# Moving an elementwise product from VectorE to GpSimd in a four-layer graph network

## The chip, the cores and the metric

The kernel runs on one core of a Trainium2 chip. The engines of a core work side by side, each on its own queue of instructions: TensorE (PE in the profile; PEld is its loading of weights), VectorE (DVE), ScalarE (ACT), GpSimd (POOL), and SyncE (SP), which here issues transfers. They meet through semaphores and through on-chip memory: SBUF, with 128 partitions, and PSUM, where TensorE leaves its results. GpSimd works on SBUF alone in this kernel. The metric is the time on the device in microseconds (us), the median of several runs; lower is better.

## The reference, cut to what matters

For 32 graphs of 512 nodes with 64 features, four layers are applied one after another, each as x = layernorm(x + layer(x, adj)). Layer 0 is a mean over neighbours; layer 1 a Chebyshev filter of order 4; layer 2 a hyperbolic attention over all pairs of nodes; layer 3 a quantile aggregation over the neighbours with an MLP. The change lies in layer 2:

```python
x_local = logmap(x_i, x_j, c)                  # for every pair of nodes
logits = einsum('bijk,ko->bijo', feats, att_W)[..., 0] + att_b[0]
att = sigmoid(logits) * adj
support_t = einsum('bij,bijd->bid', att, x_local)
return proj(expmap(support_t, x, c), c)
```

The adjacency adj is a 512 x 512 matrix for each graph with values between 0.05 and 1 at some entries and 0 elsewhere. logmap(x_i, x_j) is a weight for the pair times a combination of x_i and x_j, so layer 2 comes down to a matrix of pair weights, which is multiplied elementwise with the adjacency and with the sigmoid, and then to a product of this matrix with x.

## The kernel before, in words

A graph is one batch. Its 512 nodes lie as T = 4 tiles of P = 128 partitions, so that a 512 x 512 matrix is a tile [128, 4, 512]: four row blocks of 512 columns. Each batch goes through stages that the kernel calls lanes: `front` (line 1000: loading, transposing the adjacency into AT, layers 0 and 1), `pairs` (line 1086: layer 2's pair matrix), `tail` (from line 1211, the rest of layer 2 and its normalization), `graph` (line 996: sizes and ranks of neighbourhoods for layer 3), `gather` (line 1270: one-hot matrices and TensorE products that gather the neighbours' values), `sort` (line 1368: a sorting network of minima and maxima on VectorE, tiles SB and SH), and `head` (line 1399: quantiles, MLP, output). `head` works on two batches at once.

The order of all instructions is made while the program is built. Each helper (`tt`, `ts`, `stt` for VectorE, `act` for ScalarE, `mm` and `tr` for TensorE, `gtt` and `gts` for GpSimd) does not issue anything; it records an operation with `seq.op(engine, issue, tail, ...)`: its engine, the time that it is taken to hold the engine, and the time until its result can be used, with dependencies found from the regions that it reads and writes. Then `issue` (line 361) runs a list scheduler over all 32 batches. Each engine has a planned clock; among the operations that are ready on an engine, the one with the smallest due time goes first. The due time (`due`, line 334) is the batch number plus a number of periods, times a period of 80 us; that number is read from the knots in `STAGES` (line 1536), by how deep the operation lies in its lane's chain. So the entries of `STAGES` spread the lanes of a batch over time and set which of several lanes an engine serves first. Between operations of different engines the plan adds `HOP + LATE` (0.05 + 0.08 us). The resulting order is fixed for each engine; what waits at run time waits on semaphores. Helpers record every operation, so the profile shows the line of the helper: L514 is any `tensor_tensor` on VectorE, L521 any `scalar_tensor_tensor`, L518 any `tensor_scalar`, L550 any activation, L537 and L541 narrow arithmetic on GpSimd, L813 a power -0.5 on GpSimd, L582 an indirect gather that GpSimd issues, L1280 a fill on GpSimd. The tile names tell them apart.

In `pairs`, the matrix Q (tile pairs_Q) holds a symmetric function of each pair, L the logits and their sigmoid, Wt the final weights:

- for each row block i, TensorE writes a product into a PSUM bank; `stt` on VectorE (line 1193) multiplies it with Q[:, i] into L[:, i], and ScalarE applies the sigmoid;
- then VectorE multiplies Q in place with AT, in two instructions of 2 x 512 columns (lines 1195 to 1197). The first needs the first two row blocks of L to be done with Q, the second the last two;
- for each row block j, TensorE transposes L into a PSUM bank, and `stt` (line 1203) multiplies it with Q[:, j] into Wt[:, j];
- TensorE multiplies Wt with x and its companions, and the lane `tail` follows.

GpSimd's work in the kernel is narrow: chains of operations on tiles of 128 x 4 (one value per node) in `pairs` and `tail`, the powers for normalizations, descriptors for the gathers of layer 3, and fills of padding.

Of the kernel before, what the change touches and what calls it, by code (L numbers as in the profile page):

```python
# [15 lines left out]
OP = mybir.AluOpType  # L16
# [223 lines left out]
class Order:  # L240
# [3 lines left out]

    ENGINES = ("PE", "DVE", "ACT", "POOL", "SP")
    HOP = 0.05
    LATE = 0.08
    STAY = 58.8

    def __init__(self, nc, tc):  # L250
# [103 lines left out]
    def after(self, d, i, end, full):  # L354

        a, b = self.ops[d], self.ops[i]
        if a[0] == b[0]:
            return end + (a[2] if full and a[0] != "PE" else 0.0)
        return end + a[2] + self.HOP + self.LATE

# [109 lines left out]
def tile_adj_resnorm(ctx: ExitStack, tc: tile.TileContext, x, adj, nodemask, w1k, b1k, att_w, att_b,  # L470
                     w1, b1, w2, b2, out):
    nc = tc.nc
    B, N, D = x.shape
    T = N // P
# [16 lines left out]
    seq = Order(nc, tc)  # L491
# [7 lines left out]
    def vec(f, out, ins, one=False, scalars=(), reads=None, **kw):  # L499

        n = width(reads if reads is not None else out)
        tiles = [out] + list(ins)
        rate = 1.04e-3
        if not any(a.space == PSUM for a in tiles):
            half = all(a.dtype in (F16, BF16) for a in tiles)
            if one:
                rate = 0.26e-3 if half else 0.52e-3
            elif half:
                rate = 0.52e-3
        sc = [a for a in scalars if isinstance(a, bass.AP)]  # L510
        seq.op("DVE", 0.07 + n * rate + 0.065 * len(sc), 0.085, f, [out], list(ins) + sc)

    def tt(out, a, b, op):
        vec(lambda: nc.vector.tensor_tensor(out, a, b, op=op), out, [a, b])  # L514
# [28 lines left out]
    def act(out, a, f, bias=None, scale=1.0, accum_out=None, after=None):  # L543
        sc = [x for x in (bias, scale) if isinstance(x, bass.AP)]
        kw = {k: v for k, v in (("bias", bias), ("accum_out", accum_out)) if v is not None}
        n = width(out)
        table = "exp" if f in (AF.Ln, AF.Exp) else "sig" if f in (AF.Sigmoid, AF.Tanh) else None
        near = 0.06 if a.space == PSUM else 0.1
        seq.op("ACT", near + n * 0.83e-3 + 0.09 * len(sc) + (0.09 if accum_out is not None else 0.0),
             0.1, lambda: nc.scalar.activation(out, a, f, scale=scale, **kw), [out, accum_out], [a, after] + sc, table)  # L550
# [535 lines left out]
    def pairs(b, res):  # L1086

        mid = pools["mid"]
        AT, FL = res["AT"], res["FL"]
# [88 lines left out]
        Q = seq.tile(mid, [P, T, N], F32, "Q", 1)  # L1178
# [11 lines left out]
        for i in range(T):  # L1190
# [1 line left out]
            mm(pt, FT[:D + 3, 1, i * P:(i + 1) * P], FT[:D + 3, 2, :], start=True, stop=True)  # L1192
            stt(L[:, i, :], pt, 0.5, Q[:, i, :], op0=OP.mult, op1=OP.mult)
            act(L[:, i, :], L[:, i, :], AF.Sigmoid, bias=oo[:, i:i + 1])
        for g in range(2):
            gs = slice(2 * g, 2 * g + 2)
            tt(Q[:, gs, :], Q[:, gs, :], AT[:, gs, :], op=OP.mult)
        Wt = seq.tile(mid, [P, T, N], F32, "Wt", 1, "RW")
        for j in range(T):
            pt = bank()  # L1200
# [304 lines left out]
    def within_bounds():  # L1505

        gm, BT = pools["gm"], B * T
        seq.lane = "graph"
        p1, p2, p3 = bank(), bank(), bank()
        ge = [seq.tile(gm, [P, T, N], F16, "ge", 1, t).rearrange("p t n -> p (t n)") for t in ("nbT", "v")]  # L1510
        ge = [ge[s % 2][:, s // 2 * BT:(s // 2 + 1) * BT] for s in range(K + 1)]
        seq.lane = "check"
        m = M3.rearrange("p b t -> p (b t)")

        for s in range(K + 1):
            ts(ge[s], m, float(s), None, op0=OP.is_gt)
        for s in range(K + 1):
            mm(p1[:BT, s:s + 1], ge[s], onesP[:, 0:1], start=True, stop=True)
        cs = seq.tile(gm, [BT, K + 1], F16, "cs")
        act(cs, p1[:BT, :K + 1], AF.Copy)  # L1520
        mm(p2[:B, :K + 1], graphs[:BT, :], cs, start=True, stop=True)
        off = seq.tile(gm, [B, 2, K + 1], F16, "off")
        for i, op in enumerate((OP.is_gt, OP.is_lt)):
            tt(off[:, i, :], p2[:B, :K + 1], limits[:, i, :], op=op)
        bad = seq.tile(gm, [B, 1], F32, "bad")
        reduce(bad, off.rearrange("p i s -> p (i s)"), OP.max)
        badh = seq.tile(gm, [B, 1], F16, "badh")
        cp(badh, bad)
        mm(p3[:1, 0:1], badh, onesP[:B, 0:1], start=True, stop=True)
        ts(flag, p3[:1, 0:1], 0.0, None, op0=OP.is_gt)  # L1530
# [2 lines left out]

    STAGES = {"front": (-0.67, -0.59, -0.59, -0.4, -0.35), "pairs": (1.01, 1.02, 1.54, 1.44, 1.34),
              "tail": (2.23, 2.13, 2.56, 2.68, 2.58), "graph": (0.84, 1.06, 1.03, 1.48, 2.2),
              "gather": (2.92, 2.89, 2.92, 3.03, 2.93), "sort": (4.18, 4.47, 4.53, 5.09, 6.03),
              "head": (4.54, 5.59, 5.59, 6, 7.54), "ends": (4.04, 4.143, 4.245, 4.348, 4.45),
              "check": (1.75, 1.83, 1.91, 1.99, 2.07)}  # L1540

    nc.scalar.preload_act_table_set("natural_log_exp_and_others")
    with ExitStack() as fast:
# [44 lines left out]
        for b in range(B):  # L1588
            if b % 2 == 0:
                both = {"ends": []}  # L1590
            res = dict(both)
            seq.batch = b
            for lane, f in (("front", front), ("pairs", pairs), ("graph", stage_graph), ("gather", gather), ("sort", sort)):
                seq.lane = lane
                f(b, res)
            both["ends"].append((res["slots"][1], res["x3"][0]))
            both.update(ohm=res["ohm"], ap=res["ap"])
            if b == B - 1:
                both["spots"] = spots(both["ends"])
            if b % 2:  # L1600
                seq.lane = "head"
                head(b, both)
        within_bounds()
        seq.issue(80.0, STAGES, stay_active, 0.3)
        seq.lane = "dense"
# [141 lines left out]
    with tc.If(flagv > 0):  # L1747
        with ExitStack() as slow:
# [31 lines left out]
            for h in range(2):  # L1780
                f = cst.tile([P, D], F32, name=f"fold{h}")
                g = cst.tile([P, D], F32, name="foldg")
# [24 lines left out]
def build(inputs):  # L1807
    import numpy as np
    import concourse.bacc as bacc

    nc = bacc.Bacc("TRN2", target_bir_lowering=False, num_devices=1)
    arrays, args = {}, []
    for name in _INS:
        a = np.ascontiguousarray(inputs[name])
        if a.dtype == np.bool_:
            a = a.view(np.uint8)
        arrays[f"in_{name}_dram"] = a
        args.append(nc.dram_tensor(f"in_{name}_dram", a.shape, mybir.dt.from_np(a.dtype), kind="ExternalInput").ap())
    args.append(nc.dram_tensor("out_0_dram", inputs["x"].shape, F32, kind="ExternalOutput").ap())
    with tile.TileContext(nc) as tc:  # L1820
        tile_adj_resnorm(tc, *args)
    return nc, arrays
# [8 lines left out]
```

## Time and profile before

| what | value |
|---|---|
| median of 3 runs | 2328.9 us (2327.12 to 2333.31) |
| the profiled execution | 2326.41 us |
| its span, first to last instruction | 2324.6 us |
| mean granted TensorE clock | 0.994 |
| VectorE busy | 2115.8 us (91%) in 6952 instructions |
| TensorE busy | 2177.0 us (94%) in 18555 |
| ScalarE busy | 2033.9 us (87%) in 5818 |
| GpSimd busy | 1098.7 us (47%) in 2256 |

The profile comes from one execution. A row of a group or a tile has the line, the engine, the operation, output and inputs by the program's names, their shapes, and how often; then busy time and the mean duration, or minimum, median and maximum in ns. A row of a timeline has the start in us from the span's beginning, the duration in us, the engine, the line and the instruction; `x8` after it means that eight were merged, and a note in brackets gives idle time before it and what ended it. On VectorE an instruction is recorded as starting while the one before it is still in its last 0.08 us or so, so durations overlap a little, and the distance from start to start is what an instruction costs the stream. A window's row gives the busy time of each engine with the number of instructions, then the granted clock (1.00 is full speed) and the share and rate of the DMA engines. GpSimd's recorded spans are rough.

### The profile page before, as it was taken

Reading aid. Unit: us, or ns where it says so; the run is one execution under the profiler, and the core shown is the slowest. Engines: PE = TensorE matmul, PEld = TensorE weight load, DVE = VectorE, ACT = ScalarE, POOL = GpSimd, SP = SyncE. Lnnn points to the kernel's source line nnn. Section 1 sums busy time; section 2 is a strip of 40 time slices with the busy share of each in tenths; the row PEclk is TensorE's granted clock in tenths of the full one; section 3 lists DMA queues with packets and bytes.
Section 4 is the critical chain, followed back from the end, with each engine's and each line's share of the span. In section 5 each row is a group of like instructions: output and inputs, shape, how many; then the busy total and the mean of one; then the engine's idle time right before and its main releaser. Section 6 shows DMA issues by size and latency. Waiting matters only on the chain. (4 is left out here: it accounts for less than half of the span.)

```text
span 2324.6 us, 53396 instructions
## 1 busy us (share of the span) xinstructions
PE 2177.0 (94%) x18555; PEld 1504.3 (65%) x18555; DVE 2115.8 (91%) x6952; ACT 2033.9 (87%) x5818; POOL 1098.7 (47%) x2256
## 2 busy tenths in 40 slices
PE   6999999999999999999999999999999999999987
PEld 4666666666666666666666666666666666666655
DVE  4556999999999999999999999999999999999996
ACT  6798989999998989898989989898998989899753
POOL 1133445545464544545445554544555454454431
PEclk9999999999999999999999999999999999999999
DMA  1010001111000110100011111001111000100000
GB/s 45 21 42 12 18 22 31 27 28 31 27 18 21 34 28 26 33 26 20 22 31 28 27 33 26 19 21 32 29 27 33 26 19 17 29 15 8 13 15 14
DMA packets 131716, 57.72 MB, mean 25 GB/s; under 512 B 56140, under 2 KB 129516, under 8 KB 131436
## 3 DMA queue, kind: packets, MB, share of 16 engines
q1 hardware_dynamic: 126432, 50.09, 8.0%
q0 software_dynamic: 3840, 3.94, 0.8%
q8 instruction: 148, 2.42, 0.4%
q14 instruction: 132, 1.08, 0.2%
q10 hardware_dynamic: 1164, 0.18, 0.0%
HBM read 41.86 MB, written 12.32 MB: 23 GB/s over the span
## 5 line engine op out<-in xcount | busy, mean ns | idle before, releaser
L514 DVE TENSOR_TENSOR SB<-SB 128x92 f32<-128x92 f32 (+12 forms) x1312 | 555.3, 448 | 15.3 <-ACT SB L550 6.2
L569 PE MATMUL gather_bank<-gather_oh,tail_x3h 128*64 128x256 f16 (+5 forms) x5376 | 496.5, 318 | 7.4 <-ACT SB L550 7.1
L569 PEld LDWEIGHTS <-tail_x3h 128*64 128x64 bf16 x5376 | 333.9, 110 | 134.4 <-issue 26.2
L569 PE MATMUL pairs_bank<-pairs_FT 67*128 67x512 f32 (+7 forms) x768 | 305.6, 504 | 8.5 <-DVE pairs_L L521 2.7
L518 DVE TENSOR_SCALAR gather_oh<-graph_slot 128x256 f16<-128x256 f16 (+9 forms) x864 | 252.7, 343 | 27.1 <-PE gather_bank L569 23.5
L514 DVE TENSOR_TENSOR SH<-SH 128x288 f32<-128x288 f32 (+18 forms) x880 | 271.2, 342 | 3.8
L569 PE MATMUL front_bank<-front_AT,front_y 128*64 128x256 f32 x1536 | 190.4, 385 | 12.3 <-DVE front_y L514 11.5
L569 PEld LDWEIGHTS pairs_bank<-pairs_FT 67*128 67x128 f32 (+1 forms) x768 | 127.7, 190 | 83.8 <-issue 18.2
L582 POOL DMA_INDIRECT tail_x<-ranked,graph_spot x120 | 136.5, 1137 | 74.5 <-issue 41.4
L569 PEld LDWEIGHTS <-graph_nbT 128*128 128x128 f16 x1536 | 117.4, 98 | 78.3 <-issue 34.2
L569 PEld LDWEIGHTS front_bank<-front_AT,front_y 128*64 128x64 f32 x1536 | 108.1, 137 | 78.1 <-DVE front_y L514 22.2
L813 POOL TENSOR_TENSOR front_rs<-front_var,mhalf 128x4 f32<-128x4 f32 x64 | 81.1, 1267 | 131.4 <-DVE front_var L518 120.2
L569 PE MATMUL graph_bank<-graph_perm,graph_V 128*128 128x512 f16 x512 | 137.4, 379 | 5.3 <-DVE graph_perm L518 2.7
L569 PE MATMUL pairs_bank<-FLS,pairs_Wt 128*128 128x66 f32 x1024 | 125.6, 273 | 0.3
L514 DVE TENSOR_TENSOR pairs_RW<-pairs_RW,pairs_EX 128x640 f32<-128x640 f32 x128 | 104.7, 818 | 22.9 <-ACT pairs_EX L550 14.6
L569 PEld LDWEIGHTS pairs_bank<-FLS,pairs_Wt 128*128 128x128 f32 x1024 | 121.0, 192 | 2.5 <-DVE pairs_Wt L521 1.7
L569 PEld LDWEIGHTS <-tabs 128*128 128x128 f16 x1296 | 84.0, 98 | 48.3 <-issue 17.4
L550 ACT ACTIVATE graph_junk<-graph_bank,graph_keyh 128x512 f16<-128x512 f32 x128 | 88.0, 688 | 21.8 <-PE graph_bank L574 18.0
L569 PE MATMUL graph_bank<-UC,graph_nbT 128*128 128x512 f16 (+3 forms) x512 | 97.5, 303 | 8.4 <-ACT graph_v L550 4.1
L550 ACT ACTIVATE SB<-gather_bank 128x448 f32<-128x448 f32 (+7 forms) x288 | 89.3, 359 | 18.2 <-PE gather_bank L569 11.9
L569 PE MATMUL PA<-identf,sort_prod 128*96 128x128 f32 (+3 forms) x576 | 103.0, 282 | 1.5 <-DVE sort_prod L514 1.5
L541 POOL TENSOR_SCALAR tail_uc<-tail_un 128x4 f32<-128x4 f32 x32 | 20.7, 646 | 176.6 <-ACT tail_junk L550 170.9
(374 smaller groups left out, 6469.5 us busy)
## 6 DMA issues: line engine op xcount, KB each, us to landing
front_A<-in_adj_dram SPq DMA_DIRECT2D x128, 256.0 KB, 2.9
front_xr<-in_x_dram SPq DMA_DIRECT2D x32, 128.0 KB, 2.2
xs<-tail_x SPq DMA_DIRECT2D x32, 128.0 KB, 2.1
out_dram<-head_zo SPq DMA_DIRECT2D x31, 128.0 KB, 2.0
ranked<-sort_ap SPq DMA_DIRECT2D x30, 128.0 KB, 1.9
tail_x<-ranked,graph_spot POOLq DMA_INDIRECT x120, 2.5
out_dram<-tail_ends SPq DMA_DIRECT2D x1, 128.0 KB, 1.9
wk<-in_L_gnn_weight_dram ACTq DMA_DIRECT2D x1, 64.0 KB, 3.3
```

Source lines behind the costliest of these rows:

```text
L514: vec(lambda: nc.vector.tensor_tensor(out, a, b, op=op), out, [a, b])
L518: vec(lambda: nc.vector.tensor_scalar(out, a, s1, s2, op0=op0, **kw), out, [a], True, (s1, s2))
L541: gp(lambda: nc.gpsimd.tensor_scalar(out, a, s1, s2, op0=op0, **kw), out, [a] + [x for x in (s1, s2) if isinstance(x, bass.AP)])
L550: 0.1, lambda: nc.scalar.activation(out, a, f, scale=scale, **kw), [out, accum_out], [a, after] + sc, table)
L569: return nc.tensor.matmul(out, w, a, start=start, stop=stop)
L582: seq.op("POOL", 1.15, 2.0, lambda: nc.gpsimd.indirect_dma_start(out, None, rows, bass.IndirectOffsetOnAxis(ap=at, axis=0)), [out], [at], ...
L813: seq.op("POOL", 1.6, 0.5, lambda: nc.gpsimd.tensor_tensor(y, v, mhalf, op=OP.pow), [y], [v])
```

## The change

The product of Q with AT is made on GpSimd, in four instructions of 512 columns, one for each row block, in place of two of 1024 columns on VectorE. It is recorded in the plan with 1.15 us of issue and 0.1 us of tail. Each of the four still writes Q in place, so it follows the `stt` that makes the same row block of L, and comes ahead of the `stt` that makes the same row block of Wt. Beside it, `LATE` and the knots of all lanes but `ends` and `check` are changed.

```diff
-    LATE = 0.08
+    LATE = 0.101
...
-        for g in range(2):
-            gs = slice(2 * g, 2 * g + 2)
-            tt(Q[:, gs, :], Q[:, gs, :], AT[:, gs, :], op=OP.mult)
+        for g in range(T):
+            d = Q[:, g, :], AT[:, g, :]
+            seq.op("POOL", 1.15, 0.1, lambda d=d: nc.gpsimd.tensor_tensor(d[0], d[0], d[1], op=OP.mult), d[:1], d)
...
-    STAGES = {"front": (-0.67, -0.59, -0.59, -0.4, -0.35), "pairs": (1.01, 1.02, 1.54, 1.44, 1.34),
-              "tail": (2.23, 2.13, 2.56, 2.68, 2.58), "graph": (0.84, 1.06, 1.03, 1.48, 2.2),
-              "gather": (2.92, 2.89, 2.92, 3.03, 2.93), "sort": (4.18, 4.47, 4.53, 5.09, 6.03),
-              "head": (4.54, 5.59, 5.59, 6, 7.54), "ends": (4.04, 4.143, 4.245, 4.348, 4.45),
+    STAGES = {"front": (-0.68, -0.6, -0.36, -0.37, -0.33), "pairs": (0.99, 1.21, 1.11, 1.38, 1.44),
+              "tail": (2.07, 1.97, 2.37, 2.5, 2.4), "graph": (0.84, 1.06, 1.03, 1.81, 2.2),
+              "gather": (3.05, 2.95, 2.92, 3.16, 3.06), "sort": (3.84, 3.74, 4.19, 4.75, 5.69),
+              "head": (4.62, 5.59, 5.59, 6.24, 7.54), "ends": (4.04, 4.143, 4.245, 4.348, 4.45),
               "check": (1.75, 1.83, 1.91, 1.99, 2.07)}
```

## The prediction

> **What bounds the kernel now.** I read the page's first part, then the busy time in the steady stretch, then what each engine waits for, and last the two timelines (VectorE and GpSimd) of one place where the edited line runs.
>
> ```profile
> PE 2177.0 (94%) x18555; PEld 1504.3 (65%) x18555; DVE 2115.8 (91%) x6952; ACT 2033.9 (87%) x5818; POOL 1098.7 (47%) x2256
> ```
>
> No engine stands out over the whole span. The steady stretch alone, without filling and draining (busy time of each engine in a window):
>
> ```profile
> 330.00:2130.00 1800.00, 1712.26 (x14742) 1182.69 (x14738) 1723.28 (x5642) 1650.06 (x4758) 930.68 (x1825) 1.00 0.10 25
> ```
>
> The columns are PE, PEld, DVE, ACT, POOL. VectorE is busy 95.7%, TensorE 95.1%, ScalarE 91.7%, GpSimd 51.7%. The granted clock is 1.00. VectorE's 77 us of idle time are spread over dozens of short waits, so it sets the pace, with TensorE 11 us behind. An edit that lengthens VectorE's stream shows; one that shortens it soon meets TensorE, of whose 88 us of idle time only a part can be won.
>
> The lines that the edit touches, in the view of the tile Q:
>
> ```profile
> L521 DVE SCALAR_TENSOR_TENSOR pairs_L<-pairs_bank,pairs_Q x128: 657/682/692, 101.3 to 2179.8; 128x512 f32<-128x512 f32 x128
> L514 DVE TENSOR_TENSOR pairs_Q<-pairs_Q,front_AT x64: 1212/1225/1229, 105.3 to 2180.5; 128x1024 f32<-128x1024 f32 x64
> ```
>
> Minimum, median and maximum in ns. The product takes 1.225 us, twice a batch. And what decides the case, the two engines beside each other at the second product of a batch, VectorE first:
>
> ```profile
> 1035.66 0.68 DVE L521 SCALAR_TENSOR_TENSOR pairs_L<-pairs_bank,pairs_Q 128x512 f32<-128x512 f32 x1
> 1036.38 1.22 DVE L514 TENSOR_TENSOR pairs_Q<-pairs_Q,front_AT 128x1024 f32<-128x1024 f32 x1
> 1037.52 0.34 DVE L518 TENSOR_SCALAR graph_v<-graph_v,graph_skip 128x512 f16<-128x512 f16 x1
> ```
>
> ```profile
> 1035.89 0.21 POOL L537 TENSOR_TENSOR pairs_dn<-pairs_two,pairs_sq 128x4 f32<-128x4 f32 x1
> ...
> 1036.46 1.19 POOL L537 TENSOR_TENSOR pairs_gam<-FLS,pairs_al 128x4 f32<-128x4 f32 x1
> ```
>
> The same kind of GpSimd instruction, four columns wide, takes 0.21 us beside an instruction of VectorE that reads one input from PSUM, and 1.19 us beside one that reads two from SBUF: it ends at 1037.65, just after VectorE's product at 1037.60. I sorted all GpSimd products of 128x4 between 300 and 2200 us (without the powers of L813) by what VectorE ran when they began: 257 beside reads with a PSUM input or reductions have medians near 199 ns; 261 beside two SBUF inputs with over 300 ns to run have a median of 598 ns, and from the tenth to the fiftieth percentile they end 61 to 57 ns after VectorE's instruction. So the two engines share a way into SBUF, and the later one waits for the whole instruction of the earlier. That VectorE can be the one that waits shows at one place, with GpSimd making descriptors for a gather:
>
> ```profile
> 547.15 0.59 DVE L518 TENSOR_SCALAR graph_v<-graph_v,graph_skip 128x512 f16<-128x512 f16 x1
> ```
>
> ```profile
> 546.62 1.02 POOL L582 DMA_INDIRECT tail_x<-ranked,graph_spot  x1 [0.20 <-issue]
> ```
>
> This form has a median of 347 ns; here it took 586, ending 0.1 us after GpSimd's. What before can't show is a long read by GpSimd: its arithmetic is 4 to 8 columns wide.
>
> **The change part by part.**
>
> *Removed from VectorE.* The product starts at 1036.38 and the next instruction at 1037.52, so it holds the stream for 1.14 us: 64 x 1.14 = 73 us. This comes off the busiest engine.
>
> *Added on GpSimd: 128 products of 128x512 in f32.* No row has this. Nearest rows: GpSimd's fill of 128x512 in f16 took 514 ns (L611) and its iota of 128x512 552 ns (L619), each one pass without reading; VectorE's own 512-column two-input work takes 682 ns. Lower end one pass, 0.51 us; upper end three passes (two reads, a write) in a row, 1.54 us. I take two reads in a row with the write beside them, 2 x 0.514 = 1.03 us of holding the way into SBUF, and about 1.2 us in all with the 0.2 us that the narrow products need. GpSimd's busy time grows by 128 x 1.2 = 154 us, to some 54% of the span; it has room.
>
> [...]
>
> *VectorE held up.* In the trace's records between 300 and 2200 us, by operands, 62% of VectorE's start-to-start time goes to instructions with two SBUF inputs and 18% to those with a scalar operand from SBUF, and narrow GpSimd products waited beside both kinds (median 528 ns for the second). So 80% of its work collides. Ends per GpSimd product: 0, if VectorE's reads always go first, and 1.54 us, if the longest hold falls wholly on a waiting VectorE. I take 80% of 1.03, 0.82 us, since the rows show whole instructions being waited out: 128 x 0.82 = 105 us. Break-even with the 73 us is a hold of 73 / (128 x 0.8) = 0.71 us.
>
> [...] The trace shows the one direction for reads; no row of before shows VectorE waiting for a GpSimd read.
>
> *The new waits.* Each GpSimd product waits for its own L (it writes Q in place, which L's product reads) and for VectorE's current instruction. Behind it in GpSimd's queue stand the powers of L813 for three normalizations, the narrow chain of the next batch and the descriptors of the gather. Before, VectorE waited for GpSimd only some 6 us in all (front_rs, dn, y2), ScalarE 9.2 us for head_rs. A queue 1.2 us longer at one of these in every batch is 32 x 1.2 = 38 us at most; most have several us to spare, and I take 4. SP's queue is not passed.
>
> *When Q is ready.* The last L ends at 1036.34, and the first Wt, which needs Q, starts at 1038.48, the last at 1045.21. Four products, the first three begun after earlier L, end some 2 us after the last L. Wt goes tile by tile and also needs the sigmoid and TensorE's transposes, so this costs nothing; if that cover is gone, 1 us a batch, 32 us.
>
> *LATE and the shares.* They move priorities, not work. The refit can win at most about the idle time of VectorE in the drain (2200 to 2324 us: 124 - 102 = 22 us) and may lose as much: 0, with ends of -22 and +22. The longer LATE spaces instructions of different engines in the plan by 21 ns more; it is in the same ends.
>
> *Sum on VectorE:* -73 + 105 + 4 = +36 us. Its 77 us of idle time take some of it where a hold falls on a wait; I let a quarter go, +27. The profiled execution took 2326.4 us (span 2324.6), so 2353; it lies 2.5 us under the median of the runs, so 2356 against those.
>
> **The rivals.**
>
> *A, forecast: VectorE is held up for more than it saves.* For it: GpSimd waiting out whole instructions, the 586 ns. Own range 2337 (a hold of 0.8 us) to 2395 (1.3 us: 128 x 0.8 x 1.3 = 133, less 73, plus 4).
>
> *B, faster: VectorE's reads win and GpSimd alone waits.* For it: after a waiting GpSimd product was let go, VectorE's next two-input instruction was stretched by under 2 ns in the mean (386 cases). Against: these read four columns, which fit into the 0.1 us between two instructions. Decides if VectorE loses under 0.57 us per product (73 / 128). VectorE then saves 73, but TensorE at 95.1% and ScalarE at 91.7% come next; with TensorE at 97% the steady stretch is 1712 / 0.97 = 1765 us, -35; I put it at -10 to -45, so 2284 to 2319.
>
> *C, the two cancel:* a hold near the break-even of 0.71 us, or the idle time takes the 36 us in. 2322 to 2336.
>
> *D, GpSimd starves:* between VectorE's two-input instructions its products take 2 to 3 us each, Wt waits in VectorE's queue, and all behind it. 2 to 3 us a batch are 64 to 96 us on top: 2395 to 2425. Against it: GpSimd got in within 61 ns of VectorE's end.
>
> That the change does nothing can hardly be: VectorE sheds 64 instructions wherever the plan puts them.
>
> **How the numbers follow.** A 0.55, B 0.25, C 0.12, D 0.08. Time: A's sum, 2356. Range: C and A whole, B down to 2300 (0.10 of B's 0.25 left out below), D left out above 2395 (0.08). Under 0.3% (7 us) is about what can't be told from no change here: faster 0.27 (B and a little of C), same 0.09, slower 0.64.
>
> **What the profile after would show.** VectorE's instructions with two SBUF inputs, near the product on L, stretched by up to 1 us, or gaps before them with no semaphore behind; busy time or idle time of VectorE per batch up by about a microsecond against 1.14 x 2 saved; 128 products on GpSimd of 1.1 to 1.3 us where VectorE reads PSUM, up to 2 where it doesn't; TensorE's steady share down from 95.1%. If rows of SB and SH keep their durations beside GpSimd's products, A is wrong and B is right. I am also wrong if GpSimd's product holds the way in for far less than it lasts, or if the refit moves more than its 22 us.

## The result, and the profile after

The changed kernel takes 2485.56 us (median of 4 runs, 2481.51 to 2486.84), the kernel before 2330.14 us beside it. The ratio is 1.0664, with a 95% interval of 1.0644 to 1.0684: 155 us slower, six times the loss that was forecast and 91 us outside the range.

The first part of the page of after:

```profile
PE 2351.2 (95%) x18538; PEld 1661.3 (67%) x18538; DVE 2177.3 (88%) x6888; ACT 2051.7 (83%) x5818; POOL 1200.6 (48%) x2384
```

Two engines are busy longer, and one was not expected to be: VectorE by 62 us, though 64 products left it, and TensorE by 174 us, though the change gives it no work. The steady stretch of after (columns PE, PEld, DVE, ACT, POOL; then the granted clock):

```profile
330.00:2290.00 1960.00, 1881.91 (x14882) 1333.03 (x14881) 1800.96 (x5650) 1681.04 (x4797) 1014.27 (x1935) 0.99 0.09 23
```

TensorE is busy 96.0% here, VectorE 91.9%. Before it was VectorE that led, with 95.7%.

**VectorE and GpSimd.** The tile Q after, GpSimd's row (minimum, median, maximum in ns):

```profile
L1197 POOL TENSOR_TENSOR pairs_Q<-pairs_Q,front_AT x128: 1253/1277/2197, 100.7 to 2340.3; 128x512 f32<-128x512 f32 x128
```

One batch of after, VectorE's timeline at two of these products:

```profile
1179.19 1.50 DVE L518 TENSOR_SCALAR graph_v<-graph_v,graph_skip 128x512 f16<-128x512 f16 x1
1180.61 0.20 DVE L514 TENSOR_TENSOR SB<-SB 128x52 f32<-128x52 f32 x1
1180.73 0.68 DVE L521 SCALAR_TENSOR_TENSOR pairs_L<-pairs_bank,pairs_Q 128x512 f32<-128x512 f32 x1
1181.33 2.02 DVE L514 TENSOR_TENSOR SB<-SB 128x52 f32<-128x52 f32 x2
```

The last row merges two instructions of different widths. A window that begins behind the first of them shows the second alone:

```profile
1181.56 1.79 DVE L514 TENSOR_TENSOR SB<-SB 128x500 f32<-128x500 f32 x1
```

GpSimd's timeline at the same place:

```profile
1179.28 1.25 POOL L1197 TENSOR_TENSOR pairs_Q<-pairs_Q,front_AT 128x512 f32<-128x512 f32 x1
1181.55 1.26 POOL L1197 TENSOR_TENSOR pairs_Q<-pairs_Q,front_AT 128x512 f32<-128x512 f32 x1 [1.02 <-DVE SB L514]
```

And TensorE's (`...` for instructions left out):

```profile
1181.46 1.12 PE L569 MATMUL pairs_bank<-pairs_FT 67*128 67x512 f32 x2 [0.74 <-DVE pairs_L L521]
...
1184.45 0.77 PE L574 MATMUL front_bank<-identf,front_A 128*128 128x128 f32 x4 [1.53 <-ACT FLS L550]
```

Between the two stands ScalarE:

```profile
1183.47 0.93 ACT L550 ACTIVATE FLS<-front_bank,front_rs 128x64 f32<-128x64 f32 x4 [2.29 <-DVE FLS L514]
```

An instruction of VectorE with a median of 347 ns before takes 1.50 us, until GpSimd's product has ended at 1180.53. VectorE's instruction on L, which stands behind it, starts only at 1180.73, and TensorE waits 0.74 us for it. The 500-column instruction on SB, whose form has a median of 671 ns before, takes 1.79 us under the second product. VectorE's work on FLS behind it comes late, ScalarE waits 2.29 us for that, and TensorE 1.53 us for ScalarE. To count this I compared each instruction of VectorE with the median of its form before: in after, 115 are over 250 ns longer, by 110 us in all; before, one is.

**TensorE.** The page's rows for TensorE's largest group, the gather products, before and after:

```profile
L569 PE MATMUL gather_bank<-gather_oh,tail_x3h 128*64 128x256 f16 (+5 forms) x5376 | 496.5, 318 | 7.4 <-ACT SB L550 7.1
```

```profile
L569 PE MATMUL gather_bank<-gather_oh,tail_x3h 128*64 128x448 f16 (+5 forms) x5376 | 680.8, 318 | 1.7 <-ACT SB L550 0.7
```

The count is 5376 in both, and one product takes 318 ns in both, but the group is busy 184 us longer: the products overlap less. A merged row of each timeline shows the same shape, before first:

```profile
1030.42 1.93 PE L569 MATMUL gather_bank<-gather_oh,tail_x3h 128*64 128x340 f16 x24
```

```profile
1028.11 3.10 PE L569 MATMUL gather_bank<-gather_oh,tail_x3h 128*64 128x340 f16 x24
```

24 products of 340 columns take 1.93 us before and 3.10 us after. In the records, before they start in twelve pairs, some 13 ns apart within a pair and a pair about every 144 ns; after, most start alone, 144 ns apart, and only four times do two start within 30 ns. Each of them fills 64 of TensorE's columns (128*64 in the rows), and line 1305 sends them in turn to one half and to the other (`pt[h * D:(h + 1) * D]`, h inside). Where both halves follow each other, as in the 24 of before, two products run side by side. The built order of instructions shows what became of that: before, 79% of the gather products have one of the other half directly ahead of them, after 25%. For the products with AT in `front` it is 89% and 52%, and the group front_y of the page goes from 190.4 to 250.6 us. Where the text below gives a share of serial time, it is the distance from start to start of the gather products, divided by what one takes alone for its columns (144 ns for 340): 0.54 before, 0.76 after.

The cause lies in the due times. The two halves are two chains of accumulation in one bank, and both stand ready at once. An operation's due time is read from the knots at its depth. Where the knots rise with depth, the next product of the half that has just run is due later than the waiting one of the other half, and the halves alternate; where they are level, the program's order decides, which alternates too. Where they fall, the next product of the same half is due first, and its chain is run to the end before the other half is touched. The second stretch of `gather` rose (2.89 to 2.92) and falls in the change (2.95 to 2.92); the third of `front` rose (-0.59 to -0.4) and falls (-0.36 to -0.37).

### The profile page after: what moved, and what is told of

Read it like the earlier page. It is cut to its first block, busy times and chain, and to the rows that moved or that the text cites. A ratio compares the mean times of both kernels' runs of the same rounds, so it can differ in the third digit from the quotient of the medians.

```text
span 2485.1 us, 53632 instructions
## 1 busy us (share of the span) xinstructions
PE 2351.2 (95%) x18538; PEld 1661.3 (67%) x18538; DVE 2177.3 (88%) x6888; ACT 2051.7 (83%) x5818; POOL 1200.6 (48%) x2384
## 4 chain that ended last, share of the span: by engine, by line
PE 58%; DVE 26%; ACT 12%; POOL 2%; issue 2%; DMA 0%; POOLq 0%; DVEq 0%; ACTq 0%
PE gather_bank L569 19%; PE front_bank L569 11%; DVE SB L514 9%; PE graph_bank L569 9%; PE pairs_bank L569 8%; DVE SH L514 3%; PE front_bank L574 3%; PE pairs_bank L574 3%; DVE pairs_L L521 3%; PE head_bank L569 2%; DVE gather_oh L518 2%; PE PA L569 2%; ACT graph_dist L550 2%; DVE graph_v L518 1%; DVE pairs_Wt L521 1%
## 5 line engine op out<-in xcount | busy, mean ns | idle before, releaser
L569 PE MATMUL gather_bank<-gather_oh,tail_x3h 128*64 128x448 f16 (+5 forms) x5376 | 680.8, 318 | 1.7 <-ACT SB L550 0.7
L514 DVE TENSOR_TENSOR SB<-SB 128x92 f32<-128x92 f32 (+12 forms) x1312 | 588.2, 476 | 21.9 <-ACT SB L550 12.9
L569 PEld LDWEIGHTS <-tail_x3h 128*64 128x64 bf16 x5376 | 451.8, 110 | 178.9 <-issue 30.5
L569 PE MATMUL front_bank<-front_AT,front_y 128*64 128x256 f32 x1536 | 250.6, 384 | 2.1 <-DVE front_y L514 1.9
L1197 POOL TENSOR_TENSOR pairs_Q<-pairs_Q,front_AT 128x512 f32<-128x512 f32 x128 | 171.7, 1352 | 139.1 <-DVE pairs_L L521 95.8
L569 PEld LDWEIGHTS front_bank<-front_AT,front_y 128*64 128x64 f32 x1536 | 158.2, 136 | 67.1 <-issue 10.4
L574 PE MATMUL pairs_bank<-identf,pairs_L 128*128 128x128 f32 x512 | 98.2, 298 | 37.4 <-DVE pairs_L L521 31.6
L550 ACT ACTIVATE graph_V<-graph_bank 128x512 f16<-128x512 f32 x128 | 76.4, 597 | 64.6 <-PE graph_bank L569 64.1
L1280 POOL MEMSET SB<- 128x56 f32 (+2 forms) x96 | 11.9, 128 | 223.0 <-DVE sort_prod L514 126.7
L550 ACT ACTIVATE pairs_L<-pairs_L,pairs_oo 128x512 f32<-128x512 f32 x128 | 91.1, 724 | 32.9 <-DVE pairs_L L521 31.5
```

Of the source, the lines that this page charges most:

```text
L569: return nc.tensor.matmul(out, w, a, start=start, stop=stop)
L574: seq.op("PE", 0.12 if a.dtype == F32 else 0.06, 0.16, lambda: nc.tensor.transpose(out, a, ident), [out], [a, ident], (128, 64 if width(a) ...
L1197: seq.op("POOL", 1.15, 0.1, lambda d=d: nc.gpsimd.tensor_tensor(d[0], d[0], d[1], op=OP.mult), d[:1], d)
L1280: seq.op("POOL", 0.1, 0.06, lambda d=d: nc.gpsimd.memset(d, PAD), [d], [])
```

## The experiments

Two theories stood at the start. Theory S: the shares, which break up the pairs of halves, are most of the loss. Rival G: GpSimd's product is. By the record the experiments ran on three other chips: one for the first eight below, one for the next three, and one for the last, the run without any product. On each the kernel before, run beside them, takes 2361 to 2365 us at a granted clock of 0.982 to 0.985, so ratios to it are compared. The expectations in us were set by the first chip's 2330 us. Each of these kernels has its order planned anew, so a run differs from the kernel before in its order too, and not only in what the diff says.

**Only the product on GpSimd.** The diff is that of lines 1195 to 1197 alone.

> Only the product moves to GpSimd; LATE and the shares stay as before. Theory S (the new shares make TensorE run the two column halves of the gather and adjacency products one after the other instead of side by side; that is most of the loss): TensorE's gather products keep a start-to-start near the 0.54 of the serial time that they had before, and what is left is VectorE held up by GpSimd, -73 + 105 us and less what its idle time takes: 2340 to 2380 us. Rival G (GpSimd's product, by its hold on the way into SBUF and by the late weights behind it, is most of the loss): 2440 to 2490 us.

Measured: 2471.15 us, ratio 1.0449 (1.0398 to 1.0501). Gather products start at 0.53 of their serial time, as before. The time lies in rival G's window (carried over to the first chip by the ratio, 2435 us, it lies just under it): the product alone costs 107 us, more than S allowed. The gather products stayed paired, as S had it. VectorE is stretched by 108 us, and its share in the steady stretch falls to 90.9% (TensorE's is 91.8%, at a clock of 0.95):

```profile
330.00:2130.00 1800.00, 1652.45 (x13644) 1136.22 (x13653) 1635.98 (x5194) 1538.48 (x4404) 963.82 (x1781) 0.95 0.09 24
```

So neither engine is as busy in this run as before; more time goes into waits. Part of the loss may pass through the clock: the runs have a granted clock of 0.9635 in the median, before 0.984 beside them. As an estimate, 3.65% of 2471 us less 1.6% of 2364 us, 52 us of TensorE's full-speed time were lost to half clock beyond those of before. How many of the 107 us that is, no run tells apart.

**Only LATE and the shares.** The product stays on VectorE.

> The product stays on VectorE; LATE and the shares are those of the change. Theory S: gather products at about 0.76 of their serial time as in the changed kernel, TensorE busy some 170 us longer than before, 2440 to 2490 us. Rival G: within 25 us of before, 2305 to 2355.

Measured: 2432.46 us, ratio 1.0287 (1.0237 to 1.0338), gather products at 0.76 of their serial time, TensorE busy 2353.2 us. The shares alone cost 68 us, a time between the two theories' windows. So both halves of the change lose time, and 1.0449 x 1.0287 = 1.075 is near the 1.066 of the whole.

**The change with the halves paired again.**

```diff
-            key.append(period * (b + knots[k] + (knots[k + 1] - knots[k]) * (x - k)))
+            v = period * (b + knots[k] + (knots[k + 1] - knots[k]) * (x - k))
+            if o[0] == "PE":
+                v = max([v] + [key[d] for d in o[4] if self.ops[d][0] == "PE" and self.ops[d][6] == o[6]])
+            key.append(v)
```

> The changed kernel with one edit in the due times: an operation of TensorE is never due ahead of TensorE's operation that it depends on in its own lane and batch, so that the two halves of a product alternate again. Theory S: gather products near 0.5 of serial time, 2330 to 2380 us. Rival G: 2440 to 2490, since GpSimd's 128 products are all still there.

Measured: 2456.42 us, ratio 1.0381 (1.0329 to 1.0432). The order now has 96% of the gather products behind one of the other half, and the same 24 products of 340 columns take 1.92 us. Of the 6.6% loss 2.8% is gone; the 3.8% that remain are near the 4.5% that the product alone costs. In us the number lies in G's window; carried over by the ratio, 2419 us, it lies in neither.

**The kernel before with the halves paired.** The same edit on the kernel before, which had paired 79%.

> The kernel before with the same edit in the due times. Before had about a fifth of the gather products without the other half ahead of them. Theory S: 0.18 x 5376 products x some 80 ns = 77 us less work on TensorE, but VectorE at 95.7% comes next, so 2270 to 2325 us. If pairing the halves is worth nothing while VectorE is the bound: 2320 to 2340.

Measured: 2400.17 us, ratio 1.0149 (1.0099 to 1.0198), at a granted clock of 0.97. A miss for both: TensorE's gather products became shorter (0.49 of serial time), and the kernel slower. The profile has 20 stretches at half clock, 137 us in all, where the profile of before, taken on the other chip, has 5 with 28 us. The runs' clock was 0.9675 in the median, against 0.984 for before beside them; by the estimate used above that is 40 us of TensorE's time, and the loss was 36 us.

**GpSimd busy, but only writing.** Theory L now: GpSimd's hold on VectorE's reads is the price of its product. Rival Q: its longer queue makes later work late.

```diff
-        for g in range(2):
-            gs = slice(2 * g, 2 * g + 2)
-            tt(Q[:, gs, :], Q[:, gs, :], AT[:, gs, :], op=OP.mult)
+        for g in range(T):
+            d = Q[:, g, :], AT[:, g, :]
+            for _ in range(3):
+                seq.op("POOL", 0.38, 0.1, lambda: nc.gpsimd.memset(HOLD, 0.0), [HOLD], d)
```

> LATE and shares of before. The product of Q with the adjacency is left out; in its place GpSimd makes, in the same four places of a batch, three fills of a scratch tile of 370 columns (writes alone, some 0.38 us each by the rows of the 128x288 fill), so GpSimd is occupied as long as in the product-only run. Theory L (the hold on VectorE's reads costs most of the product-only run's 4.5%): VectorE's instructions are not stretched beyond 10 us in all, time at 0.96 to 1.01 of before. Rival Q (GpSimd's longer queue makes later work late): 1.03 to 1.05 of before.

Measured: 2383.02 us, ratio 1.0070 (1.0046 to 1.0093). GpSimd was occupied as long (161.8 us in the row below, against 171.7 us for the products of after), so the length of its queue is not what costs 4.5%:

```profile
L1198 POOL MEMSET HOLD<- 128x370 f32 x384 | 161.8, 421 | 7.6
```

The time is in L's window, but VectorE was stretched by 37 us, not under 10: 98 instructions of the form TENSOR_SCALAR and 4 casts. Of TENSOR_TENSOR, 2 were longer: one in the setup, one with an input from PSUM. In after, 46 TENSOR_SCALAR and 66 TENSOR_TENSOR are longer. So in these runs a fill of GpSimd, a write alone, held up VectorE's single-input instructions, and a product, which reads, those with two inputs as well. Nothing waits for the fills, so this run says nothing on weights that come late; but in the product-only run VectorE's waits that ended with GpSimd come to 7.2 us in all (6.0 before), and ScalarE's to 15.9 (14.2 before).

**The hold doubled.** Behind each product a second one, which nobody waits for.

```diff
+            seq.op("POOL", 1.15, 0.1, lambda d=d: nc.gpsimd.tensor_tensor(HOLD, d[1], d[1], op=OP.mult), [HOLD], d[1:])
```

> The product-only run with a second product of the same size behind each of GpSimd's 128, of the adjacency with itself into a scratch tile that nobody reads: the hold is doubled, and no weight waits for the second. Theory L: VectorE stretched by some 200 to 220 us in all instead of 108, and time at 1.08 to 1.11 of before. Rival Q, or if only the lateness of the weights counts: VectorE stretched no further, 1.04 to 1.06.

Measured: 2539.04 us, ratio 1.0731 (1.0713 to 1.0750). VectorE was stretched by 177 us: 69 us more than with one product, less than foreseen, and the time too lies between the two windows. It is 68 us more. VectorE's waits for GpSimd come to 3.6 us in all, so it isn't lateness of the weights that grew. Time that GpSimd's reads add to VectorE comes through in full here. It isn't a rule: in the writes-only run VectorE was stretched by 37 us, and against the run without any product (the last below) it lost 0.6%, some 15 us.

**The shares of two lanes alone.** The kernel before with `gather` and `front` from the change.

> The kernel before with the changed shares of two lanes alone, gather and front, which are the two whose new knots fall where the old ones rose or were level. Theory S: nearly all of the shares-only run's loss, 1.02 to 1.035 of before, with gather products at 0.75 of their serial time. Rival: the loss sits in LATE or in the other lanes: 0.99 to 1.01.

Measured: 2492.55 us, ratio 1.0539 (1.0521 to 1.0556), above the window, with gather products at 0.75 of serial time. (Two more lanes, `pairs` and `sort`, have a stretch that rose and falls in the change; but in the built program `gather` and `front` alone have chains of half-width products.) These two lanes carry the loss, and more than all of it: with the other lanes' shares and LATE it is 1.0287, so beside unpaired halves those win 2.5% back.

**Paired halves with a better planned cost.** In the plan a product with AT costs 0.88 ns a column; in the profile of before two of 256 columns take 216 ns from start to start (median), so 108 ns each, where the expectation has 98.

```diff
-            t = 0.88e-3 * n if pair else 2 * max(0.9e-3 * m, 0.93e-3 * n)
+            t = 0.42e-3 * n if pair else 2 * max(0.9e-3 * m, 0.93e-3 * n)
```

> The kernel before with paired halves (as in the run of before with that edit) and with the planned cost of the adjacency products cut from 0.88 to 0.42 ns a column, near the 98 ns that they take for 256 columns; the plan then sees more idle time on TensorE and puts 823 filling products there in place of 589. If the half-clock stretches are what took back the gain of the pairing: clock up from 0.97 to 0.98 or more, time at 0.98 to 1.00 of before. If VectorE's waits on a reordered plan are the cause: 1.01 to 1.02 again.

Measured: 2368.21 us, ratio 1.0001 (0.9982 to 1.0021), clock 0.979, 102 us at half clock. The 1.5% of the earlier run are gone. Whether the filling products or the other order did that isn't told apart by this run.

**More filling products.** In planned gaps TensorE is given products whose results nobody uses (`stay_active`). Here every gap is filled, with the product on GpSimd:

```diff
-                for _ in range(int((t - spare - fill) / 0.11)):
+                for _ in range(int((t - spare - fill) / 0.07)):
...
-        seq.issue(80.0, STAGES, stay_active, 0.3)
+        seq.issue(80.0, STAGES, stay_active, 0.0)
```

> The product-only run with more filling products on TensorE: every planned gap is filled, 1804 in place of 587. If part of that run's 4.5% comes from TensorE's clock, which fell to half for 189 us in its profile, the filling brings the clock from 0.96 to 0.98 or more and the time to 1.02 to 1.035 of before. If the clock only shows that TensorE waits for VectorE and costs little by itself: 1.04 to 1.055, the filling costing as much as it brings.

Measured: 2562.23 us, ratio 1.0831 (1.0795 to 1.0866), clock 0.979. The clock came back as foreseen (111 us at half in place of 189), and the time got worse than either case had it.

The same with paired halves and the better cost, the product on VectorE:

> The run with paired halves and the corrected planned cost, with 2475 filling products in place of 810, to win the 102 us at half clock back: 0.975 to 0.995 of before if the clock is what holds it, 1.00 to 1.02 if the filling costs what it brings.

Measured: 2522.18 us, ratio 1.0672 (1.0642 to 1.0702), clock 0.994, 31 us at half: far above both windows. Against the run without this filling it is 154 us for 1665 products. In the traces such a product takes 109 ns from start to start, so they add 181 us of work, and 71 us less at half clock give 35 us back: 146 us by this estimate. For the pair of runs with the product on GpSimd the same sum is 1217 products, 133 us, less 39 us, 94 us, and 91 us were measured. So work added to TensorE came through here, and half clock counts in these sums as half of its length; the filling brings back less than it costs.

**All shares, paired, without GpSimd's product.**

> All shares and LATE of the change, the product on VectorE, halves paired and the planned cost of the adjacency products corrected. The two-lane run was 2.5% slower than the shares-only run, so the other lanes' shares and LATE are worth something; without the lost pairing this should be level with before or better: 0.985 to 1.005. If the shares are bad for more than the pairing: 1.01 to 1.03.

Measured: 2362.70 us, ratio 0.9986 (0.9970 to 1.0002). The shares cost nothing once the halves are paired and the planned cost is corrected. This run changes both; on the kernel before the corrected cost alone moved the paired order from 1.0149 to 1.0001.

**No product at all.** The three lines are taken out and nothing stands in their place.

> LATE and shares of before; the product of Q with the adjacency is left out and nothing stands in its place, so VectorE simply has 73 us less. If time taken from VectorE comes off the end, as the prediction's sum had it: 0.968 to 0.975 of before. If it brings little because TensorE is at its own limit, while time added to VectorE by GpSimd's hold counts in full (the product-only run: 108 us of stretch, 107 us of time; the doubled hold: 69 us more of each): 0.985 to 1.00.

Measured: 2362.74 us, ratio 1.0006 (0.9996 to 1.0017). This is the end without gain of the second case: 73 us less on VectorE bring nothing in this order. The first part of its page:

```profile
PE 2204.5 (93%) x18497; PEld 1526.3 (65%) x18515; DVE 2051.3 (87%) x6888; ACT 2034.3 (86%) x5818; POOL 1052.2 (45%) x2256
```

VectorE's waits in this run, the largest first (total us, times, longest):

```profile
DVE gather_oh L518 <- PE gather_bank L569: 54.3, 38, 4.0
DVE graph_v L518 <- ACT graph_v L550: 28.6, 29, 4.3
DVE front_q L514 <- PE front_bank L574: 15.7, 6, 5.1
DVE pairs_L L521 <- PE pairs_bank L569: 13.9, 14, 2.4
```

In the profile of before the first of these was 23.5 us; VectorE's free time has become waiting, for TensorE above all. That TensorE is what holds this run is argued from these waits. The order is a new one, and the granted clock was lower, 0.9795 in the median against 0.985 beside it, which by the estimate above is 13 us of the 73; a run with the order of before held fixed was not made.

## Why the prediction was wrong

**Case A's mechanism was right.** VectorE was held up by GpSimd's reads, and the size was close: 105 us were forecast, from 1.03 us times 80%, and 110 us measured, 0.86 us for each product in place of 0.82. That it came so close is partly luck: 115 instructions were stretched for 128 products, 90% in place of 80%, by 0.96 us each in place of 1.03, and the two errors cancel. GpSimd's product took 1.28 us where 1.2 were put. Rival B, that VectorE's reads win, is refuted, and D too: GpSimd's products took 1.25 to 2.20 us, 1.28 in the median, not 2 to 3. That a wide read by GpSimd holds up VectorE was an estimate, since no row of before has such a read. In both timelines of after, VectorE's instruction ends only behind GpSimd's whole product, at 1180.69 against 1180.53 and at 1183.35 against 1182.81 (the recorded starts there lie within 0.1 us of each other, too near to say which was first). Beside a GpSimd instruction that only writes, two SBUF inputs were not held up: in the writes-only run, of 339 instructions of TENSOR_TENSOR with two SBUF inputs that ran beside a fill, none was over 250 ns longer.

**The first term failed: the 73 us taken off VectorE.** The prediction set them against the 105 us one for one. In the run without any product they are worth 0 (1.0006), and with the doubled hold the added time counts in full (69 us of stretch, 68 us of time). So the product's move costs about as much as its hold: 108 us of stretch, 107 us of time in the product-only run, with what the hold brings about in TensorE's waits and clock. Why the 73 us bring nothing stays in part open, as said at that run. The prediction saw the likely reason, TensorE at 95.1% right behind VectorE at 95.7%, and used it in rival B, but not in its own sum, where the credit should have been cut to near nothing before the debit was added. The quarter of the 36 us that was to vanish in VectorE's idle time didn't vanish either.

**The step on LATE and the shares failed outright.** It said that they "move priorities, not work", at 0 with ends of -22 and +22. They cost 2.9% alone, 68 us, by moving TensorE's two halves apart; no mechanism on TensorE was looked for. The prediction named this as a way of being wrong, if the refit moves more than its 22 us, but gave it no price. It could have been read beforehand: the plan prices these products at half time (`0.25e-3 if m == D`), the rows of before show 5376 products of 318 ns busy for only 496.5 us, so they overlap, and a falling knot reverses the due times within a lane. That the two lanes alone do it is shown by the two-lane run, and that pairing is the reason by the changed kernel with paired order (1.0381 from 1.0664, nothing else changed); the shares with paired order (0.9986 from 1.0287) agree, with the planned cost corrected beside it.

**The rest.** The two new waits were of the size put: the longer queue on GpSimd shows nowhere as a large wait of VectorE or ScalarE, and VectorE never waited for Q (VectorE's waits that ended with GpSimd are 5.6 us in all after, 6.0 before; ScalarE's 14.5 and 14.2). The ends of A's own range, 2337 and 2395, don't come from one sum: with the quarter taken off, as in the forecast, holds of 0.8 and 1.3 us give 2339 and 2377, and without it 2342 and 2393. What the profile after was to show came in part: stretched VectorE rows of up to 1 us and more, products of 1.25 us and up to 2.2. TensorE's steady share was to fall from 95.1% and rose to 96.0%.

By the ratios the whole is 1.0449 from the product times 1.0287 from the shares, less 0.8% where the two overlap. No version beat the kernel before: the best, with all shares paired and no product on GpSimd, is level with it.

## What to carry to other kernels

Where two engines are both near their limit, time added to one can come through in full, as it did here with GpSimd's reads (69 us of stretch, 68 us of time) and with TensorE's filling (146 us estimated, 154 measured), while time taken from one can bring nothing (73 us on VectorE, ratio 1.0006); price what an edit adds and what it removes apart, and don't set them off. Work moved from VectorE to GpSimd did not simply run beside VectorE's work here, where both read from SBUF: 128 products made VectorE's instructions 110 us longer. A retuned table of priorities is a change of the order on every engine: look for what depends on order, such as the pairs of half-width products here, which ran side by side where they alternated (24 in 1.93 us) and mostly one after the other where they did not (3.10 us).

## What the runs showed of the hardware that was not expected

- GpSimd's writes alone held up VectorE's TENSOR_SCALAR, not its TENSOR_TENSOR with two SBUF inputs: beside 384 fills of 0.42 us, 94 of 249 instructions of the first kind that overlap a fill are over 250 ns longer than before, and none of 339 of the second.
- In the profiles of before and after TensorE's granted clock is either 1.0 or 0.5, in stretches that are multiples of 3.413 us except where a run ends (at half: 3.413 or 6.827 us, and 10.931 and 8.579 at the ends). In the profile of before each of the 5 stretches at half clock follows 3.4 us in which TensorE was busy 69% or less (0.67, 0.64, 0.69, 0.43, 0.21). No threshold follows from this: the 3.4 us at 807.0 and at 2104.1 us, busy 0.60 and 0.49, were followed by full clock, and in the product-only run two stretches at half follow 0.72 and 0.74. A shorter stream on TensorE came with a lower clock: with paired halves and nothing else, 0.9675 in the median against 0.984 beside it, and 137 us at half. A high clock alone doesn't make a run fast: the one with a clock of 0.994 was 6.7% slower than before, by the filling that kept it up.
